# Two of every four heads' attention probabilities turned by VectorE in 32x32 blocks and joined by transfers inside SBUF

## The chip, the cores and the metric

The kernel runs on one core of a Trainium2 chip. The metric is device time in microseconds, from the start of the program to its end, as the median of several runs. A profiled execution, taken apart from these runs, gives the times of single instructions.

The engines of the core work in parallel, each through its own list of instructions in order: TensorE (PE: matrix products and transposes), VectorE (DVE), ScalarE (ACT), GpSimd (POOL) and SyncE (SP, which here only issues transfers). They meet at semaphores. Tiles live in SBUF; results of TensorE land in PSUM[...]. Both memories have 128 partitions; an instruction of the engines named works on up to 128 partitions at once[...].

## The reference

A transformer layer in float32 on 8 images of 512 tokens with 512 features. Attention has 16 heads of 32 features. Keys and queries come from a latent of 128 and have a content part for each head and a rotary part that all heads share:

```python
k = jnp.concatenate([k_c, k_rb], axis=-1)
q = jnp.concatenate([q_c, q_rb], axis=-1)
scores = jnp.einsum('bhsd,bhtd->bhst', q, k) / math.sqrt(HEAD_DIM)
attn = jax.nn.softmax(scores, axis=-1)
ctx = jnp.einsum('bhst,bhtd->bhsd', attn, v_c)
return ctx @ W_O + b_O
```

The feed-forward part has a shared network (512 to 1024 to 512, with a squared relu) for all tokens and 16 routed experts (512 to 256 to 512), of which a router picks two for each token and weighs them:

```python
h1 = jnp.einsum('th,ehi->tei', x, w_up)
a = relu2(h1) * combine[:, :, None]
routed = jnp.einsum('tei,eih->th', a, w_down)
shared = relu2(hidden_states @ shared_up) @ shared_down
```

The whole is `x = x + layernorm(attention(layernorm(x)))`, and then `x = x + layernorm(ffn(layernorm(x)))`.

## The kernel before, in words

Attention runs image by image in 16 steps each, 128 in all. Step g of image b stands for four heads (m = g // 4, heads 4m to 4m + 3) and one tile of 128 query tokens (qt = g % 4). Four steps with one m are called a group here.

A step has these parts:

- **scores** (from L324): TensorE makes four products of 128 queries by 512 keys, two to a PSUM tile of tag s (L333), of which there are two. VectorE adds the rotary scores and takes the negated maximum in one pass (L345), and ScalarE takes the exponential and its sum (L355). The probabilities `p` lie with queries on the partitions; two such tiles of four heads exist.
- **divide**: VectorE inverts the sums (L387) and GpSimd multiplies each head's probabilities by its inverse (L389).
- **keys_first**: the weighted sum needs the keys on the partitions, so each head's 128 x 512 probabilities are transposed in four 128 x 128 pieces by TensorE into PSUM (L375). VectorE copies heads 0 and 2 into the tile `pT` (L378), ScalarE heads 1 and 3 (L380). It is called for two heads at a time (a = 0, 1), and for the step before the one whose scores were just made.
- **weighted_sum** (L402), once a group, at the second step of the next group: 32 products of 32 columns of values by `pT`, one strip of 32 partitions for each head, into one PSUM tile, which ScalarE copies with the bias into `ctx`, features on partitions (L410).

Beside them a step carries other work, which `beside` (from L858) lists by g: of the same image its values (L300) and the keys and queries of the next group (L313), of the next image its load, norm, transposes and projections, and of the image before it the output projection (L421), residual and norm (from L430), router, and the rows that go to the experts. If the sum of their estimated costs is below `BUDGET` (6.4), pieces of the shared feed-forward of an earlier image are added from the list `waiting`: "up" pieces (L609, 1.72) and "down" pieces (L624, 3.43). From image 6 on the list runs out of the images before, and image 0 has none; two images' shared pieces (`LATE`) are kept for the end.

After the 8 images some further steps ("the bridge") finish the last one with what shared work is left. Then VectorE and GpSimd make the lists for the routed experts (`plan`), 79 tiles of 128 rows go through the experts (L741 to L789), and a tail adds shared and routed results, normalises and stores (L813 to L847).

The order of TensorE's instructions is written out by hand (in the routed part and the tail SP's too). The orders of VectorE, ScalarE, GpSimd and, during attention, SP are set by a scheduler that simulates the program; what each engine got in the end is a fixed list. A tile's tag with `bufs=n` has n buffers, and a new tile of the tag waits until the oldest is no longer used.

Of the kernel before, what the change touches and what calls it, by code (L numbers as in the profile page):

```python
# [38 lines left out]
def sandwich_kernel(  # L39
# [35 lines left out]
    NI = INTER // P  # L75
    NH = HID // P
    NGRP = NUM_HEADS // 4
    SCALE = 1.0 / math.sqrt(HEAD_DIM)
    GSZ = NE // N_GROUP
    HALF = S // 2  # L80
# [21 lines left out]


    def load_rows(src, b, name):
        t = sh.tile([P, NT, D], F32, tag="x", name=f"{name}_{b}", bufs=2)
# [5 lines left out]
    none = sh.tile([P, D], F32, tag="ysh", name="none", bufs=2)  # L111
    nc.vector.memset(none, 0.0)
    nc.sync.dma_start(table[NE * REGION :, :], none)

# [70 lines left out]

    slots = [const.tile([P, NT, TOP_K], I32, name=f"slots_{b}") for b in range(B)]

    which = const.tile([P, B * NT, TOP_K, NE], F32, name="which")
# [130 lines left out]


    NSTEP = NGRP * NT
    rope, probs, pTs, ctxs = {}, {}, {}, {}

    def scores(b, g):  # L324

# [36 lines left out]
            )  # L362
        probs[b, g] = pr, den

    def keys_first(b, g, a):


        m, qt = divmod(g, NT)
        if qt == 0 and a == 0:
            pTs[b, m] = at.tile([P, 4, NT, S], F32, tag="pT", name=f"pT_{b}_{m}")  # L370
        pr, _ = probs[b, g]
        for h in (2 * a, 2 * a + 1):
            pt = ps_o.tile([P, NT, P], F32, tag="o", name=f"pt_{b}_{g}_{h}")
            for c in range(NT):
                nc.tensor.transpose(pt[:, c, :], pr[:, h, c * P : (c + 1) * P], ident)  # L375
            to = pTs[b, m][:, h, :, qt * P : (qt + 1) * P]
            if h % 2 == 0:
                nc.vector.tensor_copy(to, pt)  # L378
            else:
                nc.scalar.copy(to, pt)  # L380
        if a == 1:
            del probs[b, g]

    def divide(b, g):
        pr, den = probs[b, g]
# [7 lines left out]
    def weighted_sum(b, m):  # L393


        ps = ps_o.tile([P, S], F32, tag="o", name=f"o_{b}_{m}")
        pT = pTs.pop((b, m))
        for c in range(NT):
            for h in range(4):
                r0 = h * HEAD_DIM  # L400
                col = (4 * m + h) * HEAD_DIM
                nc.tensor.matmul(  # L402
                    ps[r0 : r0 + HEAD_DIM, :],
                    lhsT=vs[b][:, c, col : col + HEAD_DIM],
                    rhs=pT[:, h, c, :],
                    start=(c == 0),
                    stop=(c == NT - 1),
                )
        ctxs[b, m] = at.tile([P, S], F32, tag="ctx", name=f"ctx_{b}_{m}", bufs=5)
        nc.scalar.activation(ctxs[b, m], ps, AF.Identity, bias=buv[:, m : m + 1])  # L410


    ao, xT, sc_, comb_, chosen_, slot_ = {}, {}, {}, {}, {}, {}
# [33 lines left out]
    def turn_f(b, i):  # L447
        if i == 0:
            late = b == B - 1
            xT[b] = sh.tile(  # L450
                [P, NK, S], F32, tag="x" if late else "xT", name=f"xT_{b}", bufs=2
            )
        turn_rows(ao[b], xT[b], i, f"f{b}")

# [120 lines left out]
    def note(b):  # L575

        mine = sb.tile([P, NT, NE], F32, tag="mine", name=f"mine2_{b}")
        r = slice(b * NT, (b + 1) * NT)
        for j in range(TOP_K):
            wh = which[:, r, j, :]  # L580
# [51 lines left out]
            finish(ysum.pop(c), c)  # L632

    def store_shared(ps, c):
        y = sh.tile([P, D], F32, tag="ysh", name=f"ysh_{c}", bufs=2)
        nc.scalar.copy(y, ps)
        nc.sync.dma_start(s_rows[c * P : (c + 1) * P, :], y)

# [11 lines left out]
        return got  # L650


    def plan():


        n = counts[B]
# [1 line left out]
        steps = sb.tile([P, NTILES + 1], F32, tag="gs", name="steps")  # L658
        nc.gpsimd.iota(steps, pattern=[[1, NTILES + 1]], base=0, channel_multiplier=0,
                       allow_small_or_imprecise_dtypes=True)  # L660
        zeros = sh.tile([P, D], F32, tag="ysh", name="zeros", bufs=2)
        nc.vector.memset(zeros, 0.0)
        pads = sb.tile([P, NE], I32, tag="base", name="pads")
        nc.vector.tensor_tensor(pads, n, eR, ALU.add)
        for e in range(NE):
# [49 lines left out]
        shift = sb.tile([P, NE], F32, tag="comb", name="shift")  # L715
        nc.vector.scalar_tensor_tensor(shift, first, float(P), eR, ALU.mult, ALU.subtract)
        shape = [P, B * NT, TOP_K, NE]
        nc.vector.tensor_tensor(
            which, which, shift.unsqueeze(1).unsqueeze(1).to_broadcast(shape), ALU.mult
        )  # L720
        moved = sb.tile([P, B * NT, TOP_K], F32, tag="gt4", name="moved")
        nc.vector.tensor_reduce(moved, which, AX.X, ALU.add)
        nc.vector.tensor_tensor(back, moved, place, ALU.add)
        return lists

# [2 lines left out]
    def routed(rt, lists):  # L728
# [48 lines left out]
        def down(j):  # L777
            py = ps_o.tile([P, D], F32, tag="o", name=f"yg_{j}")
            for i in range(NI):
                nc.tensor.matmul(  # L780
                    py,
                    lhsT=hg[j][:, i * P : (i + 1) * P],
                    rhs=sets[j % NBUF][1][:, i, :],
                    start=(i == 0),
                    stop=(i == NI - 1),
                )
            y = sh.tile([P, D], F32, tag="ysh", name=f"ysb_{j}", bufs=2)
            nc.vector.tensor_copy(y, py)
            nc.scalar.dma_start(y_rows[j * P : (j + 1) * P, :], y)  # L789

# [59 lines left out]


    LATE = 2
    BUDGET = 6.4
    BRIDGE = 7.0
    MM = 0.858
    waiting = []
# [1 line left out]
    def beside(b, g):  # L858
# [28 lines left out]
        if b < B:  # L887
            m, r = divmod(g, NT)
            if g == 0:
                add(MM, rope_scores, b, 1)  # L890
            if g == 1:
                for i in range(NT):
                    add(MM, values, b, i)
            if r == 2 and m + 1 < NGRP:
                add(2 * MM, heads, b, m + 1)
        if n < B:
            if g == 5:
                now.append((0, lambda: xs.__setitem__(n, load_rows(x, n, "x"))))
            if g == 7:
# [12 lines left out]
            if g == 15:  # L912
                add(MM, rope_scores, n, 0)
        return now

    with tc.manual_schedule(engines={mybir.EngineType.PE}):
        norm_x(0)
        for i in range(NT):
            turn_x(0, i)
        for what in ("ckv", "cq"):  # L920
            project(0, what)
        project_rope(0)
        heads(0, 0)
        rope_scores(0, 0)
        prev = None
        for b in range(B + 1):
            for g in range(NSTEP):
                if b == B and g > 12:
                    continue
                if b < B:  # L930
                    scores(b, g)
                now = beside(b, g)
                spent = sum(cost for cost, _ in now)
                at_hand = (b, g // NT - 1) if g >= NT else (b - 1, NGRP - 1)
                if g % NT == 1 and at_hand in pTs:
                    weighted_sum(*at_hand)
                    spent += 4 * MM
                if prev is not None:
                    keys_first(*prev, 0)
                if b < B:  # L940
                    divide(b, g)
                budget = BUDGET if b < B else BRIDGE if g >= 4 else 0
                while waiting and spent < budget:
                    now.append(waiting.pop(0))
                    spent += now[-1][0]
                for cost, f in now:
                    f()
# [10 lines left out]
    lists = plan()  # L958
    rt = until_tail.enter_context(tc.tile_pool(name="rt", bufs=1))
    with tc.manual_schedule(engines={mybir.EngineType.PE, mybir.EngineType.SP}):  # L960
        routed(rt, lists)
    until_tail.close()
# [62 lines left out]
```

## Time and profile before

| What | us |
|---|---|
| median of three runs | 1943.13 |
| lowest and highest of them | 1940.71, 1948.8 |
| the profiled execution | 1946.77 |
| its span, first to last instruction | 1945.1 |
| attention, from the first scores to the last | about 28.9 to 1296 |

The mean granted clock of TensorE in the profiled execution was 0.942 of full speed.

A line of the page's part on groups reads: line of the kernel, engine, operation, tile written <- tiles read, shapes and type, count | busy time in us, mean ns of one | idle time of that engine just before these instructions, and what ended most of it. In the slices each digit is a tenth of busy time (9 is 90% or more) in one fortieth of the span, 48.6 us. A line in order of time begins with start and duration in us, and ends, where the engine had been idle, with [idle time <- what ended it].

### The profile page before, as it was taken

The page shows a single profiled execution, that of the slowest core. Times are in us where ns is not written, and L with a number is a line of the kernel's source. Part 1 is how long each engine was busy: PE and PEld are TensorE (multiplying, and loading weights), DVE is VectorE, ACT ScalarE, POOL GpSimd, SP SyncE. Part 2 cuts the span into 40 slices and gives each one's busy share as a digit, 9 for nine tenths or more (in the row PEclk, how much of TensorE's full clock was granted, in tenths as well). Part 3 has the DMA queues.
Part 4 walks back from the last instruction along what each step waited for, and adds up shares of the span by engine and source line. Part 5 has one row for each costly group of instructions (what it writes and reads, how often), then busy time and mean ns, then how long its engine had stood idle before and what let it go on. Part 6 is the DMA issues. An engine that isn't in the chain of part 4 may idle for free. (4 is left out here: it accounts for less than half of the span.)

```text
span 1945.1 us, 27230 instructions
## 1 busy us (share of the span) xinstructions
PE 1726.6 (89%) x8968; PEld 1044.0 (54%) x8968; DVE 1033.1 (53%) x2695; ACT 893.3 (46%) x1977; POOL 577.7 (30%) x714
## 2 busy tenths in 40 slices
PE   7898999999999999999999989889689999996665
PEld 3444645555555545554655544445366777764443
DVE  4667745664665475446745665754522222225674
ACT  4866654654555555455545656751022222221222
POOL 1433332342324232423422353451100000006563
PEclk9999999999989998999999899889889999997787
DMA  6001111130112111211310110012456465578774
GB/s 199 1 23 44 63 58 44 55 109 33 45 54 93 49 50 39 82 49 55 105 36 23 55 66 1 22 44 70 179 184 233 131 207 180 196 266 283 261 267 153
DMA packets 125901, 199.62 MB, mean 103 GB/s; under 512 B 14145, under 2 KB 60225, under 8 KB 125761
## 3 DMA queue, kind: packets, MB, share of 16 engines
q1 hardware_dynamic: 102992, 141.50, 21.6%
q0 software_dynamic: 10240, 33.56, 4.6%
q10 hardware_dynamic: 12528, 22.81, 3.7%
q8 instruction: 73, 1.20, 0.2%
q14 instruction: 68, 0.55, 0.1%
HBM read 190.50 MB, written 65.01 MB: 131 GB/s over the span
## 5 line engine op out<-in xcount | busy, mean ns | idle before, releaser
L389 POOL TENSOR_SCALAR p<-p,rden 128x512 f32<-128x512 f32 x512 | 362.3, 726 | 788.6 <-DVE rden L387 480.7
L355 ACT ACTIVATE p<-p,nmax 128x512 f32<-128x512 f32 x512 | 363.8, 712 | 168.9 <-DVE nmax L345 161.6
L345 DVE CUSTOM_DVE_ANT_0 p<-s,rope 128x512 f32<-128x512 f32 x512 | 326.2, 686 | 93.1 <-PE s L333 69.0
L375 PEld LDWEIGHTS pt<-ident,p 128*128 128x128 f32 x2048 | 237.3, 146 | 183.7 <-issue 132.7
L609 PE MATMUL h<-xT,wsu 128*128 128x256 f32 x1024 | 251.0, 405 | 79.4 <-DMA wsu<-in_L_ffn_shared_up_dram 49.3
L375 PE MATMUL pt<-ident,p 128*128 128x128 f32 x2048 | 287.8, 285 | 25.4 <-DVE pT L378 9.1
L378 DVE COPY pT<-pt 128x512 f32<-128x512 f32 x256 | 175.1, 686 | 203.9 <-PE pt L375 197.7
L609 PEld LDWEIGHTS h<-xT,wsu 128*128 128x128 f32 x1024 | 206.2, 205 | 125.9 <-issue 50.8
L624 PE MATMUL y<-wsd,hT 128*128 128x512 f32 x512 | 228.5, 597 | 3.5 <-DVE pT L378 3.5
L380 ACT COPY pT<-pt 128x512 f32<-128x512 f32 x256 | 146.3, 576 | 112.2 <-PE pt L375 111.6
L817 POOL DMA_INDIRECT end<-y_rows,back x64 | 66.0, 1031 | 372.3 <-DMA end<-x_rows 354.3
L765 PE MATMUL hg<-xgT,set_up 128*128 128x128 f32 x1264 | 158.5, 280 | 13.3 <-DMA set_up<-in_L_ffn_w_up_dram 12.5
L333 PE MATMUL s<-k,q 32*128 32x512 f32 x1024 | 162.0, 671 | 1.9 <-DVE nmax L345 1.8
L624 PEld LDWEIGHTS y<-wsd,hT 128*128 128x128 f32 x512 | 96.6, 192 | 120.6 <-issue 111.0
L765 PEld LDWEIGHTS hg<-xgT,set_up 128*128 128x128 f32 x1264 | 150.8, 196 | 15.9 <-issue 11.8
L402 PE MATMUL o<-pT,v 128*32 128x512 f32 x1024 | 139.9, 625 | 18.7 <-DVE pT L378 17.9
L780 PE MATMUL yg<-set_down,hgT 128*128 128x512 f32 x316 | 149.7, 597 | 0.0
L774 DVE TENSOR_TENSOR hgT<-hgT 128x256 f32<-128x256 f32 x79 | 33.6, 426 | 186.4 <-ACT hgT L773 186.4
L617 DVE TENSOR_TENSOR hT<-hT 128x256 f32<-128x256 f32 x128 | 60.8, 477 | 122.4 <-ACT hT L616 117.3
L759 ACT COPY xgT<-pt_g 128x512 f32<-128x512 f32 x79 | 46.3, 586 | 161.8 <-PE pt_g L757 161.7
L616 ACT ACTIVATE hT<-h 128x256 f32<-128x256 f32 x128 | 48.5, 382 | 155.7 <-PE h L609 146.6
L421 PE MATMUL ps_ao<-wo,ctx 128*128 128x512 f32 x256 | 112.5, 593 | 0.0
(163 smaller groups left out, 1837.1 us busy)
## 6 DMA issues: line engine op xcount, KB each, us to landing
set_up<-in_L_ffn_w_up_dram SPq DMA_DIRECT2D x79, 512.0 KB
set_down<-in_L_ffn_w_down_dram SPq DMA_DIRECT2D x79, 512.0 KB
wsu<-in_L_ffn_shared_up_dram SPq DMA_DIRECT2D x64, 512.0 KB
xg<-table SPq DMA_DIRECT2D x79, 256.0 KB
y_rows<-ysb ACTq DMA_DIRECT2D x79, 256.0 KB
x<-in_L_attn_x_dram SPq DMA_DIRECT2D x32, 256.0 KB
res<-in_L_attn_x_dram SPq DMA_DIRECT2D x32, 256.0 KB
x_rows<-res SPq DMA_DIRECT2D x32, 256.0 KB
```

Of the source, the lines that this page charges most:

```text
L333: nc.tensor.matmul(tiles[-1][:, h % 2, :], lhsT=q[r0 : r0 + HEAD_DIM, qt * P : (qt + 1) * P], rhs=k[r0 : r0 + HEAD_DIM, :], start=True, st ...
L345: nc.vector.tensor_tensor_reduce(out=pr[:, h, :], in0=tiles[h // 2][:, h % 2, :], in1=rope[b, qt], scale=-1.0, scalar=3.0e38, op0=ALU.add, ...
L355: nc.scalar.activation(pr[:, h, :], pr[:, h, :], AF.Exp, bias=nmax[:, h : h + 1], scale=-1.0, accum_out=den[:, h : h + 1],)
L375: nc.tensor.transpose(pt[:, c, :], pr[:, h, c * P : (c + 1) * P], ident)
L378: nc.vector.tensor_copy(to, pt)
L380: nc.scalar.copy(to, pt)
L389: nc.gpsimd.tensor_scalar(pr[:, h, :], pr[:, h, :], rden[:, h : h + 1], 1.0, ALU.mult, ALU.mult)
L402: nc.tensor.matmul(ps[r0 : r0 + HEAD_DIM, :], lhsT=vs[b][:, c, col : col + HEAD_DIM], rhs=pT[:, h, c, :], start=(c == 0), stop=(c == NT - 1),)
L609: nc.tensor.matmul(ps[:, 0:HALF], lhsT=wsu_[b, a, i - i % NI][:, k, (i % NI) * P : (i % NI + 1) * P], rhs=xT[b][:, k, a * HALF : (a + 1) * ...
L624: nc.tensor.matmul(ysum[c], lhsT=hT[b][:, i, t * P : (t + 1) * P], rhs=wsd[:, i, :], start=(i == 0), stop=(i == NH - 1),)
L765: nc.tensor.matmul(ph[:, 0, i * P : (i + 1) * P], lhsT=sets[j % NBUF][0][:, k, i * P : (i + 1) * P], rhs=xgT[j][:, k, :], start=(k == 0), ...
L780: nc.tensor.matmul(py, lhsT=hg[j][:, i * P : (i + 1) * P], rhs=sets[j % NBUF][1][:, i, :], start=(i == 0), stop=(i == NI - 1),)
```

## The change

Heads 0 and 1 of each four are still transposed by TensorE. Heads 2 and 3 go another way:

- **blocks**: one VectorE instruction for each step turns the 32 x 32 blocks of both heads, 128 x 1024 elements, into a tile `pB`. Within a block keys are then on the partitions; but which of the four strips of 32 partitions a block lies on is still that of its queries. `pB` has one buffer, for four steps.
- **put_together**: after a group's fourth step, 16 transfers on SP's queue, for each pair of a source strip s and a strip j of the keys, copy 32 partitions of 8 x 128 elements from `pB` to `pT`. The blocks of the four steps lie side by side, so that a row of 128 elements (512 B) is contiguous. In `pT` the queries of heads 2 and 3 then stand in the order strip, step, element, and `ctx` is copied by two ScalarE instructions, of which the second puts them back in order.

The calls in the step are arranged anew. `keys_first` has two heads left and follows the scores at once; where a weighted sum is due it follows that. The weighted sum itself comes after up to `BEFORE` = 5.8 of other work instead of right after the scores. `BUDGET` falls to 5.8, and the weighted sum isn't counted in it any more. An image's values move from g = 1 to g = 4, the load of the next image from 5 to 6, its norm from 7 to 8.

SBUF space is made: the tags x and ysh have one buffer in place of two, ctx four in place of five, and the table `which` (128 x 1024) goes; `plan` computes what it needs of it anew from `place`, in a tile of the routed part's pool, and the routed results get two buffers there.

```diff
-    def keys_first(b, g, a):
+    def keys_first(b, g):
...
-        for h in (2 * a, 2 * a + 1):
+        for h in range(2):
...
+    def blocks(b, g):
+        m, qt = divmod(g, NT)
+        if qt == 0:
+            pBs[b, m] = at.tile([P, 2, NBLK, NT, HEAD_DIM], F32, tag="pB", name=f"pB_{b}_{m}")
+        pr, _ = probs[b, g]
+        nc.vector.transpose(
+            pBs[b, m][:, :, :, qt, :], pr[:, 2:4, :].rearrange("p h (n q) -> p h n q", q=HEAD_DIM)
+        )
+
+    def put_together(b, m):
+        pB = pBs.pop((b, m)).rearrange("p h (c j) t q -> p j (h c) (t q)", j=4)
+        pT = pTs[b, m][:, 2:4].rearrange("p h c x -> p (h c) x")
+        for s in range(4):
+            for j in range(4):
+                nc.sync.dma_start(
+                    pT[j * HEAD_DIM : (j + 1) * HEAD_DIM, :, s * P : (s + 1) * P],
+                    pB[s * HEAD_DIM : (s + 1) * HEAD_DIM, j],
+                )
...
-        ctxs[b, m] = at.tile([P, S], F32, tag="ctx", name=f"ctx_{b}_{m}", bufs=5)
-        nc.scalar.activation(ctxs[b, m], ps, AF.Identity, bias=buv[:, m : m + 1])
+        t = ctxs[b, m] = at.tile([P, S], F32, tag="ctx", name=f"ctx_{b}_{m}", bufs=4)
+        lo, hi = slice(0, P // 2), slice(P // 2, P)
+        nc.scalar.activation(t[lo, :], ps[lo, :], AF.Identity, bias=buv[lo, m : m + 1])
+        nc.scalar.activation(
+            t[hi, :].rearrange("p (t s q) -> p s t q", s=4, q=HEAD_DIM),
+            ps[hi, :].rearrange("p (s t q) -> p s t q", s=4, q=HEAD_DIM),
+            AF.Identity,
+            bias=buv[hi, m : m + 1],
+        )
...
-        y = sh.tile([P, D], F32, tag="ysh", name=f"ysh_{c}", bufs=2)
+        y = sh.tile([P, D], F32, tag="ysh", name=f"ysh_{c}")
...
-        zeros = sh.tile([P, D], F32, tag="ysh", name="zeros", bufs=2)
+        zeros = sh.tile([P, D], F32, tag="ysh", name="zeros")
...
-        nc.vector.tensor_tensor(
-            which, which, shift.unsqueeze(1).unsqueeze(1).to_broadcast(shape), ALU.mult
-        )
+        nc.vector.tensor_tensor(
+            over,
+            place.unsqueeze(3).to_broadcast(shape),
+            eR.unsqueeze(1).unsqueeze(1).to_broadcast(shape),
+            ALU.is_ge,
+        )
+        nc.vector.tensor_tensor(
+            over, over, by.unsqueeze(1).unsqueeze(1).to_broadcast(shape), ALU.mult
+        )
...
-    BUDGET = 6.4
+    BUDGET = 5.8
+    BEFORE = 5.8
...
+                if prev is not None:
+                    blocks(*prev)
+                    if prev[1] % NT == NT - 1:
+                        put_together(prev[0], prev[1] // NT)
                 now = beside(b, g)
-                spent = sum(cost for cost, _ in now)
+                total, spent = sum(cost for cost, _ in now), 0
                 at_hand = (b, g // NT - 1) if g >= NT else (b - 1, NGRP - 1)
-                if g % NT == 1 and at_hand in pTs:
-                    weighted_sum(*at_hand)
-                    spent += 4 * MM
-                if prev is not None:
-                    keys_first(*prev, 0)
+                behind = g % NT == 1 and at_hand in pTs
+                budget = BUDGET if b < B else BRIDGE if g >= 4 else 0
+                while waiting and total < budget:
+                    now.append(waiting.pop(0))
+                    total += now[-1][0]
+                if prev is not None and not behind:
+                    keys_first(*prev)
                 if b < B:
                     divide(b, g)
-                budget = BUDGET if b < B else BRIDGE if g >= 4 else 0
-                while waiting and spent < budget:
-                    now.append(waiting.pop(0))
-                    spent += now[-1][0]
-                for cost, f in now:
-                    f()
-                if prev is not None:
-                    keys_first(*prev, 1)
+                for cost, f in now + [(0, None)]:
+                    if behind and (spent >= BEFORE or f is None):
+                        weighted_sum(*at_hand)
+                        if prev is not None:
+                            keys_first(*prev)
+                        behind = False
+                    if f is not None:
+                        f()
+                        spent += cost
```

More of the change, by code (lines that the diff above doesn't have):

```diff
@@ L77, in sandwich_kernel @@
     NGRP = NUM_HEADS // 4
+    NBLK = S // HEAD_DIM
     SCALE = 1.0 / math.sqrt(HEAD_DIM)
@@ L104, in load_rows @@
     def load_rows(src, b, name):
-        t = sh.tile([P, NT, D], F32, tag="x", name=f"{name}_{b}", bufs=2)
+        t = sh.tile([P, NT, D], F32, tag="x", name=f"{name}_{b}")
         for i in range(NT):
@@ L110, in sandwich_kernel @@
     xs, res = {0: load_rows(x, 0, "x")}, {}
-    none = sh.tile([P, D], F32, tag="ysh", name="none", bufs=2)
+    none = sh.tile([P, D], F32, tag="ysh", name="none")
     nc.vector.memset(none, 0.0)
@@ L186, in sandwich_kernel @@
     slots = [const.tile([P, NT, TOP_K], I32, name=f"slots_{b}") for b in range(B)]
-    which = const.tile([P, B * NT, TOP_K, NE], F32, name="which")
     place = const.tile([P, B * NT, TOP_K], F32, name="place")
@@ L321, in sandwich_kernel @@
     NSTEP = NGRP * NT
-    rope, probs, pTs, ctxs = {}, {}, {}, {}
+    rope, probs, pBs, pTs, ctxs = {}, {}, {}, {}, {}
     def scores(b, g):
@@ L363, in scores @@
         probs[b, g] = pr, den
-    def keys_first(b, g, a):
+    def keys_first(b, g):
         m, qt = divmod(g, NT)
-        if qt == 0 and a == 0:
+        if qt == 0:
             pTs[b, m] = at.tile([P, 4, NT, S], F32, tag="pT", name=f"pT_{b}_{m}")
-        pr, _ = probs[b, g]
-        for h in (2 * a, 2 * a + 1):
+        pr, _ = probs.pop((b, g))
+        for h in range(2):
             pt = ps_o.tile([P, NT, P], F32, tag="o", name=f"pt_{b}_{g}_{h}")
@@ L380, in keys_first @@
                 nc.scalar.copy(to, pt)
-        if a == 1:
-            del probs[b, g]
+    def blocks(b, g):
+        m, qt = divmod(g, NT)
+        if qt == 0:
+            pBs[b, m] = at.tile([P, 2, NBLK, NT, HEAD_DIM], F32, tag="pB", name=f"pB_{b}_{m}")
[12 more added lines that the diff above has]
+                )
     def divide(b, g):
@@ L450, in turn_f @@
             xT[b] = sh.tile(
-                [P, NK, S], F32, tag="x" if late else "xT", name=f"xT_{b}", bufs=2
+                [P, NK, S], F32, tag="x" if late else "xT", name=f"xT_{b}", bufs=1 if late else 2
             )
@@ L579, in note @@
         for j in range(TOP_K):
-            wh = which[:, r, j, :]
+            wh = sb.tile([P, NT, NE], F32, tag="which", name=f"which_{b}_{j}")
             nc.vector.tensor_tensor(
@@ L650, in shared_list, with plan @@
         return got
-    def plan():
+    def plan(rt):
         n = counts[B]
@@ L713, in plan @@
         nc.vector.tensor_scalar(lists[:, 1, :], expert, float(NE - 1), None, ALU.min)
-        shift = sb.tile([P, NE], F32, tag="comb", name="shift")
-        nc.vector.scalar_tensor_tensor(shift, first, float(P), eR, ALU.mult, ALU.subtract)
+        shift = sb.tile([P, NE + 1], F32, tag="comb", name="shift")
+        nc.vector.memset(shift[:, 0:1], 0.0)
+        nc.vector.scalar_tensor_tensor(shift[:, 1:], first, float(P), eR, ALU.mult, ALU.subtract)
+        by = sb.tile([P, NE], F32, tag="chosen", name="by")
+        nc.vector.tensor_tensor(by, shift[:, 1:], shift[:, 0:NE], ALU.subtract)
         shape = [P, B * NT, TOP_K, NE]
+        over = rt.tile(shape, F32, name="over")
         nc.vector.tensor_tensor(
-            which, which, shift.unsqueeze(1).unsqueeze(1).to_broadcast(shape), ALU.mult
+            over,
[5 more added lines that the diff above has]
+            over, over, by.unsqueeze(1).unsqueeze(1).to_broadcast(shape), ALU.mult
         )
         moved = sb.tile([P, B * NT, TOP_K], F32, tag="gt4", name="moved")
-        nc.vector.tensor_reduce(moved, which, AX.X, ALU.add)
+        nc.vector.tensor_reduce(moved, over, AX.X, ALU.add)
         nc.vector.tensor_tensor(back, moved, place, ALU.add)
@@ L786, in down @@
                 )
-            y = sh.tile([P, D], F32, tag="ysh", name=f"ysb_{j}", bufs=2)
+            y = rt.tile([P, D], F32, tag="ysb", name=f"ysb_{j}", bufs=2)
             nc.vector.tensor_copy(y, py)
@@ L890, in beside @@
                 add(MM, rope_scores, b, 1)
-            if g == 1:
+            if g == 4:
                 for i in range(NT):
@@ L896, in beside @@
         if n < B:
-            if g == 5:
+            if g == 6:
                 now.append((0, lambda: xs.__setitem__(n, load_rows(x, n, "x"))))
-            if g == 7:
+            if g == 8:
                 add(0, norm_x, n)
@@ L957, in sandwich_kernel @@
     until_routed.close()
-    lists = plan()
     rt = until_tail.enter_context(tc.tile_pool(name="rt", bufs=1))
+    lists = plan(rt)
     with tc.manual_schedule(engines={mybir.EngineType.PE, mybir.EngineType.SP}):
```

## The prediction

> **What bounds the kernel now.** I read the totals and the forty slices first, then the costliest groups with what ended the idle time ahead of them, then busy time in six chosen stretches, then one step in order of time.
>
> ```profile
> PE 1726.6 (89%) x8968; PEld 1044.0 (54%) x8968; DVE 1033.1 (53%) x2695; ACT 893.3 (46%) x1977; POOL 577.7 (30%) x714
> PE   7898999999999999999999989889689999996665
> PEclk9999999999989998999999899889889999997787
> L375 PE MATMUL pt<-ident,p 128*128 128x128 f32 x2048 | 287.8, 285 | 25.4 <-DVE pT L378 9.1
> L378 DVE COPY pT<-pt 128x512 f32<-128x512 f32 x256 | 175.1, 686 | 203.9 <-PE pt L375 197.7
> L389 POOL TENSOR_SCALAR p<-p,rden 128x512 f32<-128x512 f32 x512 | 362.3, 726 | 788.6 <-DVE rden L387 480.7
> ```
>
> Over the whole span TensorE is the fullest engine; the transposes are its largest group, and it hardly idles before them. But that is a mean of unlike stages, so here is the attention by stretch: all of image 0 from its fifth step on, image 3's four groups of four steps, and four late steps of image 7. Columns are the stretch, its length, busy time of TensorE, weight loads, VectorE, ScalarE and GpSimd (with counts), granted clock, DMA share, GB/s.
>
> ```profile
> 57.80:134.10 76.30, 69.35 (x466) 35.68 (x467) 49.37 (x136) 57.52 (x139) 34.43 (x52) 1.00 0.05 15
> 477.70:523.20 45.50, 44.25 (x210) 24.88 (x209) 23.75 (x61) 23.43 (x54) 10.77 (x16) 0.96 0.09 28
> 523.20:568.90 45.70, 41.66 (x213) 23.83 (x212) 27.99 (x78) 29.19 (x59) 15.57 (x20) 0.90 0.17 58
> 568.90:614.50 45.60, 42.50 (x234) 27.82 (x234) 32.42 (x101) 23.64 (x56) 20.88 (x25) 0.98 0.35 116
> 614.50:659.60 45.10, 43.16 (x234) 23.10 (x233) 19.52 (x51) 22.12 (x52) 10.93 (x16) 1.00 0.09 30
> 1281.70:1305.50 23.80, 20.82 (x136) 12.44 (x136) 17.00 (x46) 16.94 (x42) 13.39 (x20) 0.89 0.03 12
> ```
>
> In image 3 a step lasts 11.3 us and TensorE is busy 91 to 97% of it. In images 0 and 7, which have little shared feed-forward work beside them, a step lasts 6.0 to 6.4 us. There the chain through one step's softmax is nearly as long as the step:
>
> ```profile
> 1163.54 0.69 DVE L345 CUSTOM_DVE_ANT_0 p<-s,rope 128x512 f32<-128x512 f32 x1
> ...
> 1167.24 0.18 DVE L387 RECIPROCAL rden<-den 128x4 f32<-128x4 f32 x1 [0.56 <-ACT p L355]
> ...
> 1167.58 2.69 POOL L389 TENSOR_SCALAR p<-p,rden 128x512 f32<-128x512 f32 x4 [7.67 <-PE pt L375]
> ...
> 1169.66 0.69 DVE L345 CUSTOM_DVE_ANT_0 p<-s,rope 128x512 f32<-128x512 f32 x1 [1.48 <-POOL p L389]
> ```
>
> Call the first maximum of a step N. GpSimd ends the normalisation at 1167.58 + 2.69 = 1170.27, N + 6.73. The next step's N stands at N + 6.12, ahead of that end: today VectorE owes nothing to the last two heads before it opens the next step.
>
> [...] No VectorE transpose is in the trace of before. [...]
>
> **The change part by part.** *Removed:* half of the 2048 transposes, per step 8 in about 0.97 us of TensorE, with one VectorE copy (0.686) and one ScalarE copy (0.576): 128 × 0.97 = 124 us of TensorE, 88 of VectorE, 73 of ScalarE. An image gives TensorE 16 × 0.97 = 15.5 us back.
>
> *Added to VectorE:* 128 transposes of 128x1024. The nearest row is a two-operand pass over 128x1024 in planning, which took 1.22 us[...]. I take 1.22[...]; so VectorE carries 0.53 us more a step than with the copy. Waits: the transpose reads heads 2 and 3, so it starts after N + 6.73. In the emitted VectorE order of the changed kernel it stands after the same step's reciprocal and *before the next step's four maxima*, at three steps in four (the first transpose of a group stands one step later, beside the second). Queued behind it: the maxima; after them the exponentials, the denominators, GpSimd, and TensorE's next scores through their two PSUM buffers. So a step can't be shorter than 6.73 + 1.22 + 0.10 = 8.05 us at those three places. TensorE's steps of 11.3 us cover that; the lean steps of 6.1 don't.
>
> *Added to SP:* after each fourth step 16 transfers of 32 partitions × 8 × 512 B = 131 KB, 512 in all. The four 32-partition loads at the start were issued in 1.81 us, so 16 issue in 7.2; their 256 packets an engine at the trace's 27 ns for 512 B need 6.9[...] (estimates). With some 1.5 to 2 us to completion the group lands 9 to 12 us after the last transpose; I take 11, and 20 as the bad end. The weighted sum waits for all; so does the next group's first transpose, as there is one block buffer. In steady images the weighted sum comes about 18 us after that transpose (one step, then up to 5.8 us of other work ahead of it), so 11 is hidden. In lean ones it isn't: N to N of a first step 3.9, then 11 + 3.5 (sum) + 1.0 (own transposes) + 1.3 (scores) − 3.9 = 12.9, then 8.05 twice: 32.9 a group against 25.4 (76.3/3).
>
> Weight loads and stores on SP behind a group go 7 us later, and the single store buffer makes ScalarE's next copy wait for the store: 2 us an image, inside the next figures.
>
> *Moved or small:* values from step 1 to 4 (3.4 us off a short step of image 0); VectorE's planning recomputes its comparison (one pass of 1.22) and the zero rows wait for the last shared store: +2. Two ScalarE context copies for one, 32 × 0.67 = 21 us, go where 73 left.
>
> *Sum, after minus before.* Image 0: values and two transposes less −8, three groups 98.7 − 76.3 = +22: +14. Image 1: −2 (half lean, half steady). Images 2 to 5: of 15.5 I let 8 through; the rest stays in steps 4, 5, 8 and 9, where residual, router and norms fill VectorE (27.99 and 32.42 in two stretches, in single steps it is busy as long as the step lasts) and in the store wait: 4 × −8 = −32. Image 6, whose list runs dry: +2. Image 7 and the steps after it: steps 8 to 11 +7.5, the next group's three tied steps +6.5, and the last transpose with its 16 transfers bare before the last weighted sum (1.22 + 11 − 2 hidden = +10): +24. Planning +2. [...] Together 14 − 2 − 32 + 2 + 24 + 2 + 6 = +14 us. The profiled execution is 1946.8 (span 1945.1), 3.6 over the runs' median, 1943.1; so 1957 on the median's scale.
>
> **Rivals.** *TensorE is the bound and its gain goes through.* For: 91 to 97% busy in every group of image 3. Then images 1 to 6 give 15.5 × 6 × 0.8 = −74, the lean ends cost +38: 1907. It decides when a steady image falls from 181 to below 168. Against: VectorE's full steps. *The joining is slow.* If the 16 transfers take 18.5 us rather than 11, each of six lean groups grows by 7.5 (45) and each of 24 steady ones by the 0.5 that is no longer hidden (12): 1957 + 57 = 2014[...]. For: rows are 512 B[...]. Against: a group moves 2.1 MB in 45 us, 47 GB/s, in images 1 to 6. It decides from about 14 us. *It cancels.* If the scheduler's order costs less because the maxima of a lean step slip under it, ends cost +24 rather than +38: 1943. That the turning isn't done as told can be left out: the emitted order shows 128 transposes and 512 transfers.
>
> **How the numbers follow.** Chances: forecast 0.37 (its own range 1945 to 1985), gain goes through 0.22, slow joining 0.23, cancels 0.18. No change means within 0.5% (9.7 us), about what a measurement can tell here. Slower: 0.23 + three quarters of 0.37 = 0.51; same: 0.18, from the cancelling case's middle and the forecast's lower edge; faster: 0.31. The 80% range goes from the first rival's neighbourhood, 1910, to the second's, 2015.
>
> **What would show it.** Transposes of 1.2 us, VectorE idle before them until GpSimd's normalisation: right; steps of 8 us in images 0 and 7. Image 3 at 171 to 174 us: right; below 168, the first rival. Weighted sums waiting on the joining transfers in image 3: the second. Wrong altogether if [...]TensorE steps in steady images grow for a wait I haven't named (PSUM slots behind ScalarE, say).

## The result and the profile after

The changed kernel takes 2055.4 us (median of four runs, 2053.7 to 2060.4) against 1944.1 of the kernel before beside it: a ratio of 1.0575, with a 95% interval of 1.0545 to 1.0605. It is 111 us slower; the forecast was 14, and its range ended at 2015. The profiled execution spans 2052.0 us with a mean clock of 0.888 (before: 1945.1 and 0.942).

From the page of the changed kernel, the totals, the slices, and three groups:

```profile
PE 1667.1 (81%) x7944; PEld 938.8 (46%) x7944; DVE 1121.0 (55%) x2698; ACT 853.0 (42%) x1891; POOL 575.8 (28%) x714
PE   6577879979987997998799677756959999995665
PEclk9787899979989997999899787867979999998888
L637 PE MATMUL h<-xT,wsu 128*128 128x256 f32 x1024 | 259.9, 415 | 126.2 <-DMA wsu<-in_L_ffn_shared_up_dram 92.1
L389 DVE STREAM_TRANSPOSE pB<-p 128x1024 f32<-128x1024 f32 x128 | 157.0, 1238 | 219.1 <-POOL p L410 164.5
L423 PE MATMUL o<-pT,v 128*32 128x512 f32 x1024 | 156.6, 697 | 91.5 <-DMA pT<-pB 90.7
```

TensorE has 1024 matmuls fewer, but is busy only 59.5 us less, not 124: at a lower clock (0.888 against 0.942) what remains takes longer. In both traces a product of the weighted sum takes 0.59 us (median) at full clock and 1.06 at half; the 1024 of them are busy for 156.6 us, where they were for 139.9 before. It idles most in the first slices and around the 27th, the images with little shared work. The turning waits for GpSimd for 164 us, the weighted sums for the joining for 91, and the shared network for its weights for 92 (49 before).

In order of time, the end of a group in image 7, where little shared work stands beside the steps:

```profile
1366.45 1.25 DVE L389 STREAM_TRANSPOSE pB<-p 128x1024 f32<-128x1024 f32 x1 [3.84 <-POOL p L410]
...
1367.83 11.03 SPq L400 DMA_DIRECT2D pT<-pB  x16
...
1368.40 1.29 PE L423 MATMUL o<-pT,v 128*32 128x512 f32 x4
1368.50 0.69 DVE L345 CUSTOM_DVE_ANT_0 p<-s,rope 128x512 f32<-128x512 f32 x1
...
1381.42 2.37 DVE L389 STREAM_TRANSPOSE pB<-p 128x1024 f32<-128x1024 f32 x2 [8.99 <-DMA pT<-pB]
1381.43 5.87 PE L423 MATMUL o<-pT,v 128*32 128x512 f32 x28 [11.74 <-DMA pT<-pB]
```

The last turning ends at 1367.70, and the sum gets its probabilities at 1381.43: the join takes 13.7 us. TensorE stands for 11.7 of them, and the 28 products behind the wait take 5.87 us at a granted clock of 0.61, where a whole sum of 32 takes 3.6 at 1.00 in image 3. VectorE's maxima (1368.50) stand behind a turning that had waited 3.84 us for GpSimd.

And in image 3, step 9, first SP's queue, then TensorE:

```profile
617.61 11.14 SPq L400 DMA_DIRECT2D pT<-pB  x16
628.85 11.49 SPq L622 DMA_DIRECT2D wsu<-in_L_ffn_shared_up_dram  x3
```

```profile
634.09 7.58 PE L637 MATMUL h<-xT,wsu 128*128 128x256 f32 x24 [9.96 <-DMA wsu<-in_L_ffn_shared_up_dram]
641.60 3.64 PE L423 MATMUL o<-pT,v 128*32 128x512 f32 x32
```

Here the weighted sum doesn't wait for its join; but the weights of the shared network, issued behind the 16 transfers, come 10 us too late.

By images, from first maximum to the next image's first maximum in the profiled executions, and for image 7 to its last step's, the experiments of the next section included:

| kernel | time, us | image 0 | 1 | 3 | 6 | 7 | clock |
|---|---|---|---|---|---|---|---|
| before | 1940 to 1944 | 103.9 | 163.5 | 181.9 | 156.3 | 121.4 | 0.942 |
| split_on_pe: new order, all by TensorE | 1965.1 | 102.2 | 170.6 | 186.9 | 155.6 | 120.4 | 0.936 |
| no_turn: half of the transposing left out | 1844.8 | 91.5 | 151.4 | 167.6 | 144.8 | 109.6 | 0.933 |
| no_join: and the turning put in | 1959.9 | 110.8 | 162.7 | 177.2 | 161.9 | 132.2 | 0.903 |
| after: and the joining put in | 2055.4 | 134.4 | 180.5 | 181.7 | 168.4 | 150.9 | 0.888 |

Read downwards, the change comes apart into four terms: the order and the buffers +23, the freed TensorE −120, the turning +115, the joining +95, each as it is in this order of putting them in. (no_turn, no_join and, below, no_join_pinned ran once each; the kernel before spread over 1932 to 1956 us in all its runs, so a term may be off by some 10 us.)

By their pages TensorE is busy for 1726.6, 1728.9, 1599.4, 1660.8 and 1667.1 us in these five kernels. With the same matmuls the turning lengthens that by 61 us, so about half of its 115 us is TensorE taking longer over the same work, and the rest is standing; the joining lengthens it by 6, so nearly all of its 95 us is standing.

### The profile page after: what moved, and what is told of

The parts are those of the page before. It is cut to its first block, busy times and chain, and to the rows that moved or that the text cites. A ratio compares the mean times of both kernels' runs of the same rounds, so it can differ in the third digit from the quotient of the medians.

```text
span 2052.0 us, 25886 instructions
## 1 busy us (share of the span) xinstructions
PE 1667.1 (81%) x7944; PEld 938.8 (46%) x7944; DVE 1121.0 (55%) x2698; ACT 853.0 (42%) x1891; POOL 575.8 (28%) x714
## 4 chain that ended last, share of the span: by engine, by line
PE 51%; DVE 11%; SPq 9%; DMA 8%; ACT 7%; POOL 7%; issue 6%; POOLq 0%; DVEq 0%; ACTq 0%
PE y L652 10%; PE h L637 8%; SPq L400 7%; PE o L423 6%; PE hg L804 6%; PE yg L819 6%; ACT p L355 6%; POOL p L410 5%; DVE p L345 4%; PE s L333 4%; DMA wsu<-in_L_ffn_shared_up_dram 3%; PE pt L375 2%; DVE pB L389 2%; DMA pT<-pB 2%; PE pt_g L796 1%
## 5 line engine op out<-in xcount | busy, mean ns | idle before, releaser
L637 PE MATMUL h<-xT,wsu 128*128 128x256 f32 x1024 | 259.9, 415 | 126.2 <-DMA wsu<-in_L_ffn_shared_up_dram 92.1
L637 PEld LDWEIGHTS h<-xT,wsu 128*128 128x128 f32 x1024 | 211.4, 210 | 179.2 <-issue 97.1
L389 DVE STREAM_TRANSPOSE pB<-p 128x1024 f32<-128x1024 f32 x128 | 157.0, 1238 | 219.1 <-POOL p L410 164.5
L423 PE MATMUL o<-pT,v 128*32 128x512 f32 x1024 | 156.6, 697 | 91.5 <-DMA pT<-pB 90.7
L333 PE MATMUL s<-k,q 32*128 32x512 f32 x1024 | 174.3, 698 | 15.6 <-DVE nmax L345 15.4
L375 PEld LDWEIGHTS pt<-ident,p 128*128 128x128 f32 x1024 | 119.6, 150 | 144.9 <-issue 74.0
L375 PE MATMUL pt<-ident,p 128*128 128x128 f32 x1024 | 154.8, 296 | 33.7 <-POOL p L410 31.2
L423 PEld LDWEIGHTS o<-pT,v 128*32 128x32 f32 x1024 | 38.6, 124 | 205.0 <-issue 191.6
L378 DVE COPY pT<-pt 128x512 f32<-128x512 f32 x128 | 87.5, 683 | 78.2 <-PE pt L375 78.2
```

What stands on the lines that cost most here:

```text
L333: nc.tensor.matmul(tiles[-1][:, h % 2, :], lhsT=q[r0 : r0 + HEAD_DIM, qt * P : (qt + 1) * P], rhs=k[r0 : r0 + HEAD_DIM, :], start=True, st ...
L389: nc.vector.transpose(pBs[b, m][:, :, :, qt, :], pr[:, 2:4, :].rearrange("p h (n q) -> p h n q", q=HEAD_DIM))
L423: nc.tensor.matmul(ps[r0 : r0 + HEAD_DIM, :], lhsT=vs[b][:, c, col : col + HEAD_DIM], rhs=pT[:, h, c, :], start=(c == 0), stop=(c == NT - 1),)
L637: nc.tensor.matmul(ps[:, 0:HALF], lhsT=wsu_[b, a, i - i % NI][:, k, (i % NI) * P : (i % NI + 1) * P], rhs=xT[b][:, k, a * HALF : (a + 1) * ...
```

## The experiments

Theory A held the joining responsible, theory B the turning, theory C the new order and buffers. The kernel before, run beside them each time, lay at 1940 to 1944 us.

**no_join**, the joining taken out:

```diff
-                    rhs=pT[:, h, c, :],
+                    rhs=pT[:, h % 2, c, :],
...
-                    if prev[1] % NT == NT - 1:
-                        put_together(prev[0], prev[1] // NT)
```

> The changed kernel without its 512 joining transfers; the weighted sums of heads 2 and 3 read the transposed probabilities of heads 0 and 1 instead, so that part of the computation is left out. VectorE still turns the blocks, at the same places. Theory A, the joining transfers are the cost (weighted sums wait for them, and weight loads stand behind them on SP): 1905 to 1925 us, a steady image 168 to 173 us, no long step 9. Theory B, VectorE's turning ahead of the next maxima and the colder clock are the cost: 2010 us or more. Theory C, the new order, budget and single buffers are the cost: 2010 us or more too.

Measured 1959.9, which is in none of the ranges. The joining costs 95 us, 67 of them in images 0, 1, 6 and 7, and step 9 of image 3 falls from 20.9 to 12.2 us. But without any of it the kernel still isn't faster than before: A alone falls.

**all_on_pe** and **split_on_pe**, the new order with all four heads transposed by TensorE; in the first all at once, in the second in two halves as before. The edit of split_on_pe:

```diff
-        for h in range(2):
+        for h in (2 * a, 2 * a + 1):
...
-                if prev is not None:
-                    blocks(*prev)
-                    if prev[1] % NT == NT - 1:
-                        put_together(prev[0], prev[1] // NT)
...
+                if prev is not None:
+                    keys_first(*prev, 1)
```

> The changed kernel's order, budget, moved work and buffer numbers, but all four heads transposed by TensorE: no blocks, no joining transfers. Theory A: 1935 to 1955 us, as before within a per cent. Theory C, order and buffers cost: 2000 us or more. If the new order is itself a gain that the turning hides: below 1930 us.

> As all_on_pe, but with the second pair of heads transposed at the end of the step as in the kernel before, so that the PSUM copies aren't bunched. If bunching made all_on_pe slow: 1940 to 1960 us, and a steady image 180 to 184. If the new order, budget or single buffers cost by themselves: 1975 us or more.

all_on_pe took 2095.8 us (ratio 1.0781, 1.0744 to 1.0819), split_on_pe 1965.1 (1.0115, 1.0093 to 1.0136). The first is no measure of the order. Four transposed heads in a row need four PSUM buffers, all that their tag has, and TensorE waits for VectorE's copies, as the list of waits of all_on_pe has it (engine, what it waited for, us in total, times, longest):

```profile
PE pt L375 <- DVE pT L378: 41.7, 24, 3.4
```

In split_on_pe this wait is 13.1 us. Other products that need a buffer wait for the same copies: with them it is 141 us in all_on_pe and 64 in split_on_pe, so 77 of the 130 us between the two. What is left in split_on_pe, 1.2%, is the order, the budget and the buffers.

**split_buffers**, the last with two buffers for x and the shared rows and five for ctx:

```diff
-        y = sh.tile([P, D], F32, tag="ysh", name=f"ysh_{c}")
+        y = sh.tile([P, D], F32, tag="ysh", name=f"ysh_{c}", bufs=2)
```

> As split_on_pe (all heads by TensorE, new order and budget), with the buffers of the kernel before: two for x and for the shared rows, five for ctx. If single buffers make its loss of 25 us: 1938 to 1950 us. If order and budget do: 1957 us or more.

1958.5 us, ratio 1.0079 (1.0056 to 1.0103). Two thirds of the loss are order and budget; the rest would be the buffers, though the two intervals just overlap.

**no_turn**, no_join without VectorE's turning:

```diff
-                if prev is not None:
-                    blocks(*prev)
```

> As no_join (heads 2 and 3 take the probabilities of heads 0 and 1 in the weighted sum, no joining transfers), and VectorE's turning left out as well: half of the transposing is left out and nothing takes its place. If the turning costs where it stands: 1920 to 1940 us against 1960 for no_join, lean steps at 6.2. If it is hidden: 1950 us or more. The distance to the kernel before is then what the freed TensorE time is worth in this order.

1844.8 us, beyond both expectations. The turning costs 115 us in no_join although VectorE is busy for 56% of the span. The stretches are image 0 and image 3, in each kernel; columns as in the prediction. First no_turn, then no_join:

```profile
28.80:120.20 91.40, 79.31 (x440) 36.01 (x436) 58.36 (x174) 73.85 (x176) 41.03 (x61) 0.91 0.10 35
441.80:609.40 167.60, 154.80 (x758) 82.19 (x757) 96.73 (x272) 93.98 (x210) 60.09 (x76) 0.97 0.18 63
```

```profile
28.50:139.30 110.80, 89.39 (x440) 38.20 (x436) 75.11 (x190) 73.84 (x176) 41.02 (x61) 0.85 0.09 30
479.20:656.40 177.20, 159.27 (x757) 83.29 (x758) 111.88 (x287) 93.67 (x210) 58.97 (x76) 0.94 0.18 60
```

With the same matmuls, TensorE is busy 10 us longer in image 0, at a clock of 0.85 against 0.91, and stands for 21.4 us in place of 12.1.

**no_join_pinned**, no_join with the turning pinned in VectorE's order behind the next step's maxima:

```diff
-        nc.vector.transpose(
+        tc.keep_in_program_order(nc.vector.transpose(
```

> As no_join (heads 2 and 3 take the probabilities of heads 0 and 1, no transfers), with VectorE's turning pinned behind the next step's maxima. no_turn against no_join says that turning costs 115 us. If its place ahead of the maxima costs that, most of it comes back: 1850 to 1890 us. If VectorE's time does, wherever it stands: 1930 us or more.

1918.6: between the two. The place is worth 41 us, nearly all in lean images (image 0: 110.8 to 94.5; image 3: 177.2 and 177.8). Two lean steps of it in order of time:

```profile
71.45 1.24 DVE L389 STREAM_TRANSPOSE pB<-p 128x1024 f32<-128x1024 f32 x1
...
76.24 1.25 DVE L389 STREAM_TRANSPOSE pB<-p 128x1024 f32<-128x1024 f32 x1 [0.47 <-POOL p L410]
```

They are 4.8 us apart, where no_join's lean steps last 8.0. The other 74 us, against no_turn, stay in both places that VectorE's 1.24 us had. Behind the maxima the PSUM copies come later instead: TensorE's wait ahead of the shared network in step 15 of image 3, which ScalarE's copy ends here, is 2.2 us in place of 1.3. How the 74 us add up step by step is not shown.

**turn_after_max**, the same pin with the joining kept:

> The changed kernel with VectorE's turning pinned behind the next step's four maxima, so that the maxima no longer wait for GpSimd's end. If the place of the turning costs: lean steps of 8.0 us fall to 6.2 to 6.5 at about a dozen places, steady images lose 1 to 2 us each, 2025 to 2040 us. If that place is hidden or the join, starting later, takes it back: 2048 to 2060 us.

2108.2 us (1.0864, 1.0835 to 1.0892), slower by 53 and outside both ranges. Image 0's lean steps fall to 4.3 to 6.4 us, but the last turning of each group ends later, and with it the join. First the changed kernel's line in the list of waits, then that of turn_after_max:

```profile
PE o L423 <- DMA pT<-pB: 90.7, 10, 12.4
```

```profile
PE o L423 <- DMA pT<-pB: 112.6, 17, 13.3
```

(Another 34.3 us of waits of the sum stand in this list under the stores of x_rows, which run beside the join.) In image 3 a sum now begins 8 to 12 us after the last turning at two groups of four, where it began after 15 to 25. So 13.7 us of join were hidden in steady images with little to spare, and the early place of the turning was what hid them.

**long_rows**, **alternate** and **join_by_two** ask what makes the join long. Both tiles laid out for rows of 4 KB; then the transfers in an order that alternates between halves of the partitions; then half of them on ScalarE's queue:

```diff
-                    pT[j * HEAD_DIM : (j + 1) * HEAD_DIM, :, s * P : (s + 1) * P],
+                    pT[j * HEAD_DIM : (j + 1) * HEAD_DIM, s * 8 * P : (s + 1) * 8 * P],
...
-        for s in range(4):
-            for j in range(4):
+        for t in range(4):
+            for s, j in ((0, t), (2, t ^ 2), (1, t ^ 1), (3, t ^ 3)):
...
-                nc.sync.dma_start(
+                (nc.scalar if j % 2 else nc.sync).dma_start(
```

> The same bytes and the same 16 transfers a group, but both tiles laid out so that each transfer is 32 rows of 4 KB in place of 256 rows of 512 B. If a transfer's 0.69 us on SP goes by its rows, 0.4 us each, 6.5 us a group, joined about 9 us after the last transpose in place of 13.7: lean steps 4 to 5 us shorter at some 10 places, step 9 of the steady images 5 us shorter, 1975 to 1995 us. If it goes by the transfer, whatever its rows: 2045 to 2060 us.

> As long_rows, with the same 16 transfers of a group issued in another order: sources go 0, 2, 1, 3 and targets alternate likewise, so that neighbours in the queue use different halves of the partitions. [...] a group issues in 6.5 to 8 us and the time is 2005 to 2020 us. If each transfer costs SP 0.63 us anyway: 2030 to 2042 us, as long_rows.

> As long_rows, with half of a group's 16 transfers issued by ScalarE's queue and half by SP's. If a queue's 0.63 us for each transfer bounds the join: it ends 7 to 8 us after the last transpose in place of 12.6, and with the weight loads freed earlier 1995 to 2015 us. If the transfer engines bound it, or ScalarE's exponentials wait behind its issues: 2025 us or more.

2036.3 (1.0482, 1.0435 to 1.0528), 2035.0 (1.0487, 1.0466 to 1.0507) and 2084.3 us (1.0731, 1.071 to 1.0753). Rows an eighth as many save 19 us, which lies between the two ranges; the other order nothing; the second queue costs 48. The transfer view of one group's join gives queue, packets, MB, and the packets' time as a share of 16 engines. In the changed kernel over 12.0 us, in long_rows over 10.5, in join_by_two over 9.9:

```profile
q1 hardware_dynamic: 4352, 2.10, 74.0%
```

```profile
q1 hardware_dynamic: 768, 2.10, 87.9%
```

```profile
q10 hardware_dynamic: 384, 1.05, 47.8%
q1 hardware_dynamic: 384, 1.05, 45.4%
```

A group is 4096 packets of 512 B and 256 small ones, or 512 of 4 KB and 256 small ones. 0.74 × 12.0 × 16 / 4352 is 33 ns a packet; 0.879 × 10.5 × 16 us over 512 long ones is 288 ns: 15 and 14 GB/s an engine, with either row. With 512 B rows the engines are busy 74% of the time; whether the gaps come with SP's issues, 0.69 us each, or between packets is not shown. Long rows fill them to 88%, two queues to 93%, and there is little more to be had: by an estimate from these shares (0.88 × 10.5 and 0.93 × 9.9 us) the transfer engines alone need some 9 us for 2.1 MB. Why a packet inside SBUF takes that long stays open. The three groups moved 175, 200 and 212 GB/s, and neighbours in the queue on different halves of the partitions didn't change the time (2035.0 us against 2036.3), so which partitions a transfer touches is not shown to be the bound. And with ScalarE issuing, its own work queues behind the issues (the list names the transfers; in order of time the copy stands right behind an issue):

```profile
ACT pT L380 <- DMA pT<-pB: 108.9, 20, 7.2
```

**wsu_on_act**, the weights of the shared network on ScalarE's queue, but for the two late images:

```diff
-            nc.sync.dma_start(wsu, cols.rearrange("(c p) i -> p c i", p=P))
+            (nc.sync if b >= B - LATE else nc.scalar).dma_start(wsu, ...)
```

> The changed kernel with the shared up weights of the attention part loaded through ScalarE's queue, so that they no longer stand behind the joining transfers on SP. Theory A with the queue as the cause in steady images: step 9 falls from 21 to about 11 us in images 1 to 6, 1995 to 2010 us; images 0 and 7 unchanged. If the loads are late for another reason (their buffer, the transfer engines being full): 2045 us or more.

2053.4 us (1.057, 1.052 to 1.062): nothing. Step 9 of image 3 falls only from 20.9 to 19.2. The weights come earlier, and now the sum waits; SP's queue, then TensorE:

```profile
615.26 15.49 SPq L400 DMA_DIRECT2D pT<-pB  x16
```

```profile
634.90 6.58 PE L423 MATMUL o<-pT,v 128*32 128x512 f32 x28 [3.30 <-DMA pT<-pB]
```

The 16 issues stretch from 11.1 to 15.5 us while three weight loads of 512 KB go beside them. In the changed kernel TensorE waits 9.96 us for the weights there, here 3.30 us for the join; what the transfers share is not shown.

**steady**: turning and joining (long rows) in images 2 to 5 alone, the others with the calls and the budget of the kernel before; **steady_pinned**: there with the turning tied behind the next step's first maximum (in the list that came out it stands behind the second):

```diff
+    turned = lambda b: 2 <= b <= 5
...
-        nc.vector.transpose(
+        ins = nc.vector.transpose(
...
+            tc.add_manual_dep(
+                ins.ins, first_max[-1], mybir.DependencyInfo(
+                    mybir.DependencyClass.NoSync, mybir.DependencyReason.DATA
+                ), reason="after the first maximum",
+            )
```

> Turning and joining (long rows) in images 2 to 5 alone, where the shared work is full; images 0, 1, 6 and 7 with all heads by TensorE in the calls of the kernel before; buffers as in the changed kernel. If the loss lies in the lean images and steady ones break even: 1938 to 1955 us. If the steady images lose by themselves: 1965 us or more. A gain would be below 1930.

> As steady, with the turning pinned behind the next step's second maximum (in place of the scheduler's place ahead of all four). If the turning's place costs some 10 us in each steady image: 1915 to 1935 us. If the later join takes it back: within 8 us of steady or slower.

steady took 1943.2 us, ratio 1.0008 (0.9997 to 1.0019): as before, image by image (image 3: 181.3). steady_pinned took 1930.5, ratio 0.9942 (0.9923 to 0.9962): 12 us less than before, 3 to 4 in each of the four images (image 3: 177.9). Of the versions that compute the whole layer it is the fastest, 0.6% below the kernel before.

**skip_second** and **skip_second_wide** leave the second group of a steady image to TensorE, where join and weights meet, and add the steady groups of images 1 and 6:

```diff
-    turned = lambda b: 2 <= b <= 5
+    turned = lambda b, m: m != 1 and 2 <= b <= 5
```

> As steady_pinned, with the second group of four steps in images 2 to 5 left to TensorE (turned: groups 1, 3 and 4). If the joining costs there because it meets the shared weight loads of steps 8 to 10: step 9 falls from 18 to 12 us, 3.9 us of transposes come back, 1912 to 1926 us. If the collision moves to another group: 1928 us or more.

> As skip_second, and groups 3 and 4 of image 1 and group 1 of image 6, which are steady too, turned by VectorE. 2 to 3 us a group off: 4 to 9 us below skip_second if they gain as in images 2 to 5; equal within 3 us if not.

1939.4 (0.9987, 0.9973 to 1.0002) and 1938.8 us (0.9983, 0.997 to 0.9996), 8 to 9 us behind steady_pinned. Step 9 does fall, from 18.2 to 10.6 us, and TensorE stands for 1.5 us of it in place of 5.1. But steps 5 to 7 grow by 3.4, 2.4 and 1.3. These three steps together, first in steady_pinned, then in skip_second:

```profile
534.50:558.10 23.60, 19.20 (x116) 11.87 (x108) 16.44 (x43) 18.79 (x39) 5.41 (x8) 0.85 0.19 63
535.90:566.60 30.70, 25.47 (x151) 15.75 (x142) 16.96 (x48) 23.03 (x46) 6.45 (x10) 0.78 0.17 56
```

Of 7.1 us more, 6.3 are busy time of TensorE: 24 transposes that came back, some products of the weighted sum, and a lower clock (0.78 against 0.85). Image 3 stays at 178.0: what the wait gave back, TensorE's own work took.

## Why the prediction was wrong

**What held.** The direction, which had a chance of 0.51, and the bounds named for it. The turning takes 1.24 us (1.22 assumed). Lean steps last 8.0 us (8.05), held by GpSimd's end and the maxima queued behind the turning; no_join_pinned shows that place as the cause. The weights behind the join on SP were seen, and that the clock would cost something too. But +14 was a small difference of large terms, so the right direction is in part luck; every stage came out higher than forecast. Changes in us, from the profiled executions:

| stage | forecast | measured |
|---|---|---|
| image 0 | +14 | +30.5 |
| image 1 | −2 | +17.0 |
| images 2 to 5 | −32 | +7.2 |
| image 6 | +2 | +12.1 |
| image 7 and all that follows, with planning and clock | +32 | +41.3 |

**Step "of 15.5 I let 8 through" in a steady image.** This is the largest miss. Images 2 to 5 changed by +3.5, −0.2, +3.1 and +0.8, where −8 each was forecast; image 3 stood at 181.7, not at the 171 to 174 named as the sign of being right. In image 3 the freeing of TensorE was sized too low (15.5, measured 19.3 from split_on_pe to no_turn), but three costs were left small: the order +5.0, for which the sum has no term; VectorE's 1.24 us a step +9.6, which I charged with 0.53 us at the few full steps only; and the join with the late weights +4.5, of which I had 2: together −0.2. VectorE's share of a mean, 63% in image 3, said nothing of this: what the turning adds stands ahead of the next maxima or of the copies that free PSUM.

**Step "I take 11" for the join.** It lasts 13.7: 1.3 us until the first packet, then 12 us of engines that move 15 GB/s each. I had 7.2 us for the 16 issues, which took 11.0, and 27 ns for a packet against 33 measured. The 12 us at the upper end of my range was an estimate that nothing in the trace of before showed; the 1.5 to 2 us to completion fit the smallest transfers in the trace of after, of 0.1 KB, which landed 1.6 and 1.9 us after their issue. The point from which I let the slow joining decide, "about 14 us", was nearly reached: that rival, at 2014, was the nearer one. It isn't confirmed, though: by its own sign the sums of image 3 would wait for the join, and they don't. Its arithmetic had 45 us for six lean groups; 10 groups waited, of images 0, 6 and 7 (the last of image 0 within image 1), and images 0, 1, 6 and 7 lost 67 to the joining.

**Step "12.9" for a lean step with a sum.** Measured 16.6 to 20.7 in image 0. The join gives 2.7 of the difference, the sum after the wait, at 5.9 us in place of 3.5, another 2.4. Lean groups of image 0 took 37.5, 42.4 and 34.3 us (114 together), not 98.7.

**Step "+ 6", the clock.** The mean clock fell from 0.942 to 0.888. In these two traces it is granted at 1.00 or 0.50, so about 226 us ran at half speed before and 460 after. My +6 was an estimate, from two stretches of 3.4 us at half speed and small queue delays. Weighted with the clock granted at each moment, TensorE's busy time falls from 1651 to 1539 us, by 112 in place of the 59.5: so some 53 of the 65 us that it didn't lose are clock, a cost within the terms above rather than a separate one. The trace of before doesn't show that half speed goes by long waits: in its attention 25 stretches of 3.4 or 6.8 us run at half speed, but TensorE stands for longer than the shorter of these only twice (4.21 and 3.92 us). One such stretch and the 3.4 us ahead of it, columns as in the prediction:

```profile
365.50:368.90 3.40, 1.33 (x10) 1.03 (x11) 1.86 (x6) 3.40 (x10) 0.82 (x2) 1.00 0.00 0
368.90:372.30 3.40, 3.40 (x8) 1.85 (x8) 0.00 (x0) 2.00 (x4) 1.88 (x3) 0.51 0.02 5
```

Other stretches follow 3.4 us in which TensorE was busy for 19 to 100%. So stretches at half speed followed busy windows as well as idle ones here; what sets the clock is not shown.

The rival that TensorE's gain goes through is refuted as it stood, but no_turn shows how large that gain is: 95 us below the kernel before beside it, if nothing had taken its place.

## What to carry to other kernels

Taking work from the fullest engine pays only as far as the engine that gets it has room at the moments that others wait on. Leave the work out altogether first, and then put the substitutes in one by one: the 120 us freed here were nearly spent by the turning alone (115), and the joining (95) came on top. A substitute that needs an in-order engine to wait for the end of a chain should stand behind that engine's next urgent instruction, but each step it moves back also starts its transfers later; both sides were seen here (41 us gained in no_join_pinned, 53 lost in turn_after_max), and the best of the places tried lay between. An operation with no row in the trace, such as a transfer inside SBUF, is best given a range that reaches well below the rate of the transfers that are shown (33 ns a packet here, where others of that size had taken 27).

## What the runs showed of the hardware

Transfers within SBUF, from 32 partitions to 32 others, moved 14 to 15 GB/s on each of 16 engines, with rows of 512 B (33 ns each) as with rows of 4 KB (288 ns each); a second queue raised the engines' share of busy time from 88 to 93% and shortened a group from 10.5 to 9.9 us. Beside weight loads from HBM the same 16 issues went from 11.1 to 15.5 us. VectorE's transpose of 128x1024 in 32x32 blocks took 1.24 us, where an ordinary pass over as many elements took 1.22 in the kernel before. In the attention of the kernel before, TensorE's clock was half of full speed in 25 stretches of 3.4 or 6.8 us, though TensorE stood for longer than the shorter of these only twice (4.21 and 3.92 us).
